# A convolution's reload moved one step behind its store, at two places of an LSTM, and the first chunk's work moved ahead in attention's opening

## The chip, the cores and the metric

The kernel runs on one core of one Trainium2 chip. A core has five engines with instruction queues of their own: PE (TensorE, matrix products), DVE (VectorE), ACT (ScalarE), POOL (GpSimd) and SP (SyncE, which here only issues transfers between the core's memory and DRAM). The metric is the device time of one execution in microseconds (us); less is better.

## The reference

The input x is [128, 64, 256]: 128 graphs of 64 nodes with 256 features, and one 64x64 adjacency for all. Four layers follow each other, each of the form x = x + layer(relu(layernorm(x))):

```
layer 0: two-layer perceptron with batch norms, after an aggregation with the normalized adjacency
layer 1: two graph convolutions
           h = relu(adj @ (h @ Wg0 + bg0)) ;  h = relu(adj @ (h @ Wg1 + bg1))
         then for p = 1, 2, 3, 4: an LSTM over windows of p nodes; its last state
         replaces the last node of each window
           g = x_t @ Wih.T + h @ Whh.T + bias ; c = sig(f) c + sig(i) tanh(g) ; h = sig(o) tanh(c)
layer 2: causal attention with one head, mask adj, output projection
layer 3: attention with four heads, masked where adj is 0
```

All is float32.

## The kernel before

**Tiling.** The 128 x 64 rows are cut into 16 chunks of 512 rows (NCH = 16), two chunks make a superchunk (SUP = 2), so there are 8 superchunks, sc = 0 to 7. Layer 0 runs first over all chunks. The stage in the middle runs over superchunks: the LSTMs of superchunk sc stand in it (`lstms`), and around them, as fillers, the convolutions of the next superchunk, the residual of the last one and the first steps of attention's norm. The last stage runs over chunks: attention of layer 2 for chunk c beside layer 3 for chunks c-1 to c-3.

**The order is written by hand.** In the middle stage the LSTM is a generator that stops at numbered marks: p=1 has marks 0 to 3, p=2 has 4 to 7, p=3 has 8 to 13, p=4 has 14 to 21, with half marks between. Tables of numbers say at which mark each step of a filler is taken: `FIRST` and `CONV` for the convolutions of the next superchunk (`FIRST` while sc = 0), `BEGUN` for the first steps of those of the superchunk after that (while sc is 0 to 5), `LATE` and `AHEAD` for the norm of attention. Each table has one tuple per chunk of the superchunk. So `BEGUN[0]` opens the convolution of its first chunk at marks 11, 11.5, ... and `BEGUN[1]` that of its second at 17.5, 19, 21.

**The convolution's filler** (`convolutions`). First step: the batch norm's scale and shift (L918). Second step: DVE transposes the chunk by 32x32 blocks into `ym` (L1009), a transfer stores it to DRAM as `far_y` (`put`, L261), four transfers reload it in another arrangement into `cv` (`get`, L268), and one loads x into `xs` (L1016); `xs` takes the place of `ym`. Third step: DVE adds both (`add_squares`, L298). Then come the layer norm's statistics in two steps (L195, L196, with POOL's rsqrt at L99, L100 and `nmr` at L202, L203), its application on ACT (L210), the aggregation, the product v (L936), the bound (L942), the product u (L950), the second aggregation and the copy to `hT` (L961).

**The LSTM's weights.** Sets of 896 KB (`wset`, one for each p and gate q) are reloaded for each superchunk, two at a time, into six buffers. `load_sets(2)` (L905) stands twice in the last step of each p: just behind the half mark (11.5 in p=3, 19.5 in p=4) and before the last mark (13 and 21). The two sets loaded behind mark 11.5 are those of p=4 for q=3 and q=1. The order of first products in p=4 is q=0, q=2 and q=3 (L1134; q=3 writes tile `x`).

**One queue for transfers.** All transfers of this stage are issued by SyncE in the order in which the program lists them. The transfer's wait (for a store's landing, or for a buffer to come free) is a wait of SyncE, so what is listed behind it is issued later.

**The single LSTM, p=1.** Three gates at once, products L1369, adds on DVE L1393, activations on ACT L1374 and L1382, copies L1389.

**Attention's opening.** The last stage begins with a string of step names, `FIRST` (a second use of that name), which interleaves chunks 0 to 3: `score2` (L1719, L1722, then `mx` L1642 and POOL's subtraction L1643), `exp2` (L1729), `divide2` (sum L1647, reciprocal L1652, product L1653), `turn2` (transposes L1662, copy L1666), `v2a` and `v2b` (L1521, L1523), `q2` (L1528, L1697) and `copyq2` (L1702), `out2` (products L1750, adds into `xs` L1753), `keep` (store `far_x`) and `back` (its reload), `weights3` (load of `w_sb`, whose memory is that of chunk 0's v), `norm3`, `apply3` (L187), `chan3` (transposes `tc_n` L240), `q3`, `k3` (L1528 with `w_sb`), `score3` (L1904, L1910), and for the last two chunks of layer 1 the residual `res1` (transposes `hm` L1309, store and reload `far_h`, add L298) and the reordering `pair1` (store and reload `far_n`). `load3+1` is the reload `hT` of chunk 1 for layer 3, whose first product is `Z` (L1825).

Of the kernel before, what the change touches and what calls it, by code (L numbers as in the profile page):

```python
# [19 lines left out]
def kernel(  # L20
# [169 lines left out]
    def norm_halves(src, name):  # L190

        st = small.tile([P, NJ, 6], F32, tag=f"ln_st{NJ}", name=f"st_{name}")
        mv = small.tile([P, NJ, 2], F32, tag=f"ln_mv{NJ}", name=f"mv_{name}")
        for j in range(NJ):
            nc.vector.bn_stats(st[:, j, :], src[:, j, :])  # L195
            nc.vector.bn_aggr(mv[:, j, :], st[:, j, :])  # L196
            if j == NJ // 2 - 1:
                yield
        rstd = small.tile([P, NJ], F32, tag=f"ln_rstd{NJ}", name=f"rstd_{name}")
        nmr = small.tile([P, NJ], F32, tag=f"ln_nmr{NJ}", name=f"nmr_{name}")  # L200
        rsqrt(rstd, mv[:, :, 1], EPS)
        nc.gpsimd.tensor_tensor(nmr, mv[:, :, 0], rstd, OP.mult)  # L202
        nc.gpsimd.tensor_scalar(nmr, nmr, -1.0, None, op0=OP.mult)  # L203
        yield rstd, nmr

    def apply_halves(dst, src, stats, name):

        rstd, nmr = stats
        for j in range(NJ):
            nc.scalar.activation(dst[:, j, :], src[:, j, :], AF.Relu, bias=nmr[:, j : j + 1],  # L210
                                 scale=rstd[:, j : j + 1])
            if j % 2:
                yield
# [4 lines left out]
    def aggregate(src, mat, name):  # L218

        banks = [bank(f"agg{e}_{name}").rearrange("p (k j t) -> p k j t", j=NJ, t=T) for e in range(2)]
        for j in range(NJ):
            for k in range(KD):
                for i in range(2):
                    for e in range(2):
                        f = slice(k * P + i * T, k * P + (i + 1) * T)
                        nc.tensor.matmul(banks[e][half(i), k, j, :], src[half(e), j, f],
                                         mat[half(e), half(e)], start=True, stop=True)
        return [ps.rearrange("p k j t -> p (k j) t") for ps in banks]  # L230
# [27 lines left out]
    def put(mid, name, tag="far", bufs=12):  # L258

        far = dram.tile([P, Q, CH * KD // Q], F32, tag=tag, name=f"far_{name}", bufs=bufs)  # L260
        nc.sync.dma_start(far, mid)  # L261
        return far

    def get(dst, far):

        src = far.rearrange("(a t) b n -> b t a n", a=Q)
        for b in range(Q):
            nc.sync.dma_start(dst[b * 32 : (b + 1) * 32], src[b])  # L268
# [21 lines left out]
    def add_squares(dst, base, src):  # L290

        for h in range(2):
            q = slice(h * Q // 2, (h + 1) * Q // 2)

            def part(a):
                return a.rearrange("p j (k q c) -> p q (j k) c", k=KD, q=Q)[:, q]

            nc.vector.tensor_add(part(dst), part(base), src[:, q].rearrange("p q (n c) -> p q n c", c=32))  # L298
# [613 lines left out]
    def scaled(y, c, m):  # L912
        one = slice(m, m + 1)
        if c == 0 and not m or c == 1:
            nc.scalar.activation(y[:, m, :], z2[c][:, m, :], AF.Identity, bias=sh2[:, one],
                                 scale=sc2[:, one])
        else:
            nc.vector.tensor_scalar(y[:, m, :], z2[c][:, m, :], sc2[:, one], sh2[:, one],  # L918
                                    op0=OP.mult, op1=OP.add)
# [4 lines left out]
    def conv_tile(c):  # L924

        t = shared(f"cv_{c}")
        return t.rearrange("p (k n) -> p k n", k=KD), t.rearrange("p (j d) -> p j d", d=D)

    def by_batch(agg):
        return agg.rearrange("p k (j e t) -> p e (k j) t", e=2, t=T)  # L930

    def product_v(c, agg):
        banks = [bank(f"v1_{c}_{m}") for m in range(KD)]
        for m in range(KD):
            for k in range(KD):
                nc.tensor.matmul(banks[m], wg0_sb[:, k, m * P : (m + 1) * P], agg[:, k, :],  # L936
                                 start=(k == 0), stop=(k == KD - 1))
        return banks

    def bounded(v, banks):  # L940
        for m in range(KD):
            nc.vector.tensor_tensor(v[:, m, :].rearrange("p (j n) -> p j n", n=P),  # L942
                                    banks[m].rearrange("p (j n) -> p j n", n=P),
                                    nc1[:, m, None, :].to_broadcast([P, NJ, P]), OP.max)

    def product_u(c, v):
        banks = [bank(f"u1_{c}_{t}").rearrange("p (j d) -> p j d", d=D) for t in range(NJ // 2)]
        for j in range(NJ):
            for k in range(KD):
                nc.tensor.matmul(banks[j // 2][:, j % 2, :], v[:, k, j * P : (j + 1) * P],  # L950
                                 wg1_sb[:, k, :], start=(k == 0), stop=(k == KD - 1))
        return banks

    def biased(u, banks):
        for t, ps in enumerate(banks):
            nc.vector.tensor_add(u[:, 2 * t : 2 * t + 2, :], ps, c2[:, None, :].to_broadcast([P, 2, D]))
# [44 lines left out]
    def convolutions(c):  # L1001

        y, h = conv_tile(c)
        for m in range(KD):
            scaled(y, c, m)
        yield
        mid = res.tile([P, Q, CH * KD // Q], F32, tag=f"r{c}", name=f"ym_{c}")
        for k in range(KD):
            nc.vector.transpose(  # L1009
                mid.rearrange("p b (j k c) -> p k j b c", j=NJ, k=KD)[:, k],  # L1010
                y[:, k, :].rearrange("p (j b t) -> p j b t", b=Q, t=32))
        far = put(mid, f"y{c}")
        dst = y.rearrange("p k (q n) -> p (k q) n", q=2)
        get(dst, far)
        xs[c] = res.tile([P, NJ, D], F32, tag=f"r{c}", name=f"xs_{c}")
        nc.sync.dma_start(xs[c], xr[c])  # L1016
        yield
        add_squares(xs[c], xs[c], dst)
        yield
        for stats in norm_halves(xs[c], f"b{c}"):  # L1020
            yield
        yield from apply_halves(h, xs[c], stats, f"b{c}")
        banks = aggregate(h, adjt_bd, f"b{c}")
        yield
        for e, ps in enumerate(banks):
            nc.vector.tensor_copy(by_batch(y)[:, e], ps)
        yield
        banks = product_v(c, y)
        yield
        bounded(y, banks)  # L1030
        yield
        banks = product_u(c, y)
        yield
        biased(h, banks)
        yield
        banks = aggregate(h, adjt_bd, f"c{c}")
        yield
        for e, ps in enumerate(banks):
            to_hT(c, e, ps)
            yield  # L1040
# [514 lines left out]
    EARLY = 0, 3, 5, 7, 9, 9, 13, 15  # L1555
    RESIDUAL = (0, 6, 9), (5.5, 7, 9.5)
    CONV = (3, 4, 5, 5.5, 7, 8, 9, 10, 10), (5, 5, 6, 9.5, 11, 11.5, 13, 14, 15, 15.5, 17, 18, 20)
    BEGUN = (11, 11.5, 14.5, 17, 17, 20, 21), (17.5, 19, 21)
    RESIDUAL_LAST = (0, 4, 5.5), (3, 5, 9)
    FIRST = (1, 1, 2, 2, 3, 4, 4, 5, 5.5, 7, 8, 9, 10, 10), (2, 3, 4.5, 5, 5, 6, 9.5, 11, 11.5, 13, 14, 15, 15.5, 17, 18, 20)  # L1560
    AHEAD = (9, 10), (10, 11)
    LATE = (4.5, 4.5, 5.5, 9, 19.5), (9.5, 9.5, 11, 12, 21)
    LATEST = (4.5, 4.5, 5.5, 9, 9.5), (9.5, 9.5, 10, 11, 11.5)
# [27 lines left out]
    with tc.manual_schedule(engines={mybir.EngineType.PE, mybir.EngineType.DVE, mybir.EngineType.Pool,  # L1591
# [4 lines left out]
        for sc in range(last + 1):  # L1596
            todo = {}

            def units(places, unit):
                for n in places:  # L1600
                    todo.setdefault(n, []).append(unit)


            if sc < last:
                for i in range(SUP):
                    units((CONV if sc else FIRST)[i], convs[(sc + 1) * SUP + i])
                new_hT(sc + 1)
# [11 lines left out]
            if sc + 1 < last:  # L1619
                for i in range(SUP):  # L1620
                    units(BEGUN[i], convs[(sc + 2) * SUP + i])
            if sc == last:
# [406 lines left out]
    def store(c, t):  # L2029
# [3 lines left out]
        for r in range(2):  # L2033
# [16 lines left out]

    FIRST = """load2+2 score2+0 exp2+0 res1+14 v2a+1 v2b+1 score2+1 divide2+0 load2+3 q2+2 copyq2+2
               turn2+0 exp2+1 v2a+2 out2+0 keep+0 divide2+1 norm3+0 v2b+2 turn2+1 score2+2 res1+15 out2+1
               keep+1 exp2+2 weights3+0 divide2+2 apply3+0 back+0 chan3+0 res1+14 turn2+2 res1+15 norm3+1
               q30+0 k30+0 out2+2 keep+2 res1+14 q31+0 res1+15 k31+0 apply3+1 pair1+14 pair1+14 square3+1
               score3+0 norm3+2 pair1+15 pair1+15 v3a+0 load3+1 v3b+0"""
    LAST = """exp3-2 sum3-2 load3+0 divide3-2 qa-1 q5-1 c11-1 v3a-1 qb-1 c12-1 qc-1 turn3-2 qd-1 out3-2
              score3-1 q30+0 store-2 back-1 k30+0 back+0 exp3-1 q31+0 sum3-1 k31+0 divide3-1 score3h+0
              v3b-1 exp3a+0 sum3a+0 turn3-1 exp3b+0 v3a+0 divide3a+0 out3-1 sum3b+0 divide3b+0 store-1  # L2060
# [8 lines left out]
    with tc.manual_schedule(engines={mybir.EngineType.PE, mybir.EngineType.DVE,  # L2069
                                     mybir.EngineType.Activation, mybir.EngineType.Pool,  # L2070
                                     mybir.EngineType.SP}):
        run(FIRST, 0)
        close_l1r()
# [61 lines left out]
```

## Time and profile before

| what | value |
|---|---|
| time, median of 3 runs | 1904.61 us (1903.06 to 1906.54) |
| span of the profiled execution | 1901.8 us |
| PE busy | 1845.0 us, 97% of the span |
| DVE, ACT, POOL busy | 1323.1, 1052.1, 613.0 us |
| chain that ended last, share of PE | 85% |
| layer 1's LSTM stage | about 274 to 1521 us |
| attention's opening | about 1521 to 1565 us |
| `wset` loads | 96, of 896 KB, median 8.2 us from issue to landing |
| `far_y`, `cv`, `xs` transfers | median 2.6, 3.0 and 4.5 us to landing |

Lines of the timeline read: start in us, busy time in us, engine, line of the kernel, operation, output <- inputs, shapes, count; in brackets how long the engine was idle before and what ended that. "SPq" is the issue of a transfer by SyncE. "PEld" is TensorE's weight load, which overlaps its products. A wait is put down to the releaser that came last by the profile.

### The profile page before, as it was taken

The page shows a single profiled execution, that of the slowest core. Times are in us where ns is not written, and L with a number is a line of the kernel's source. Part 1 is how long each engine was busy: PE and PEld are TensorE (multiplying, and loading weights), DVE is VectorE, ACT ScalarE, POOL GpSimd, SP SyncE. Part 2 cuts the span into 40 slices and gives each one's busy share as a digit, 9 for nine tenths or more (in the row PEclk, how much of TensorE's full clock was granted, in tenths as well). Part 3 has the DMA queues.
Part 4 walks back from the last instruction along what each step waited for, and adds up shares of the span by engine and source line. Part 5 has one row for each costly group of instructions (what it writes and reads, how often), then busy time and mean ns, then how long its engine had stood idle before and what let it go on. Part 6 is the DMA issues. An engine that isn't in the chain of part 4 may idle for free.

```text
span 1901.8 us, 40668 instructions
## 1 busy us (share of the span) xinstructions
PE 1845.0 (97%) x15463; PEld 1519.0 (80%) x15463; DVE 1323.1 (70%) x3408; ACT 1052.1 (55%) x2499; POOL 613.0 (32%) x856
## 2 busy tenths in 40 slices
PE   8999988999999999999999999999999989999998
PEld 6877856987987888799698788789979956777776
DVE  6768846667667777776776776876667666776776
ACT  5766545546547456564664655656556534444453
POOL 5856632223213322222422322332222213332232
PEclk9999999999999999999999999999999989999999
DMA  3224551123433343242343334333244155454433
GB/s 114 79 66 145 207 205 53 62 109 122 149 118 123 111 156 118 89 130 87 133 156 112 145 122 145 145 103 131 95 123 145 35 161 145 139 152 144 135 112 112
DMA packets 113410, 234.48 MB, mean 123 GB/s; under 512 B 11712, under 2 KB 77120, under 8 KB 113216
## 3 DMA queue, kind: packets, MB, share of 16 engines
q1 hardware_dynamic: 112320, 230.02, 36.4%
q8 instruction: 123, 2.02, 0.4%
q0 software_dynamic: 320, 1.05, 0.2%
q10 hardware_dynamic: 576, 0.82, 0.1%
q14 instruction: 71, 0.58, 0.1%
HBM read 164.21 MB, written 67.63 MB: 122 GB/s over the span
## 4 chain that ended last, share of the span: by engine, by line
PE 85%; DVE 6%; DMA 3%; ACT 2%; POOL 2%; issue 1%; SPq 0%; DVEq 0%; ACTq 0%; POOLq 0%
PE x L1187 21%; PE z L1187 11%; PE y L1187 6%; PE v L1521 5%; PE y L1134 4%; PE x L1369 4%; PE y L1369 3%; PE u L950 3%; PE x L1134 3%; PE p_q L1528 3%; PE X L1825 3%; PE X L437 2%; DMA wset<-wfar 2%; PE X L513 2%; PE v L936 2%; PE z L1134 2%
## 5 line engine op out<-in xcount | busy, mean ns | idle before, releaser
L1102 ACT ACTIVATE l_gates<-l_gates,bias 128x256 f32<-128x256 f32 (+4 forms) x528 | 238.1, 498 | 217.3 <-DVE l_gates L1196 109.9
L1187 PE MATMUL x<-xd,wset 128*128 128x128 f32 (+2 forms) x1152 | 255.0, 303 | 0.8 <-ACT l_gates L1193 0.8
L1187 PE MATMUL x<-l_hd,wset 128*128 128x128 f32 (+2 forms) x1152 | 254.5, 303 | 0.0
L1253 POOL TENSOR_TENSOR l_gates<-l_gates 128x512 f32<-128x512 f32 (+2 forms) x48 | 75.3, 1569 | 397.8 <-ACT l_gates L1102 397.8
L1187 PEld LDWEIGHTS x<-xd,wset 128*128 128x128 f32 x1152 | 187.7, 191 | 6.5 <-issue 1.4
L1187 PEld LDWEIGHTS x<-l_hd,wset 128*128 128x128 f32 x1152 | 187.8, 191 | 5.0
L1196 DVE TENSOR_TENSOR l_gates<-l_gates,x 128x128 f32<-128x128 f32 (+2 forms) x384 | 121.1, 321 | 97.4 <-PE x L1187 94.4
L1196 DVE TENSOR_TENSOR l_gates<-l_gates,z 128x128 f32<-128x128 f32 (+2 forms) x384 | 102.3, 318 | 106.8 <-PE z L1187 104.7
L1187 PE MATMUL z<-l_hs,wset 128*128 128x128 f32 (+2 forms) x768 | 147.1, 304 | 0.7 <-DVE l_hs L1111 0.7
L1187 PE MATMUL z<-hT,wset 128*128 128x128 f32 (+2 forms) x768 | 146.2, 303 | 0.0
L1193 ACT COPY l_gates<-y 128x128 f32<-128x128 f32 (+2 forms) x192 | 53.2, 290 | 137.6 <-PE y L1187 131.3
L1187 PEld LDWEIGHTS z<-l_hs,wset 128*128 128x128 f32 x768 | 116.8, 191 | 5.8 <-DVE l_hs L1111 2.5
L1187 PEld LDWEIGHTS z<-hT,wset 128*128 128x128 f32 x768 | 117.1, 191 | 3.3
L1102 ACT ACTIVATE l_gates<-x,bias 128x128 f32<-128x128 f32 (+2 forms) x216 | 84.8, 393 | 28.9 <-PE x L1187 26.2
L1187 PE MATMUL x<-hT,wset 128*128 128x128 f32 (+2 forms) x384 | 85.8, 305 | 0.0
L1187 PE MATMUL x<-l_hs,wset 128*128 128x128 f32 (+2 forms) x384 | 84.8, 303 | 0.0
L327 POOL TENSOR_TENSOR xd<-hT 128x128 f32<-128x128 f32 (+2 forms) x72 | 42.7, 594 | 126.6 <-DVE hT L1113 114.3
L1187 PE MATMUL y<-l_hd,wset 128*128 128x128 f32 (+2 forms) x384 | 83.2, 309 | 0.0
L1187 PE MATMUL y<-xd,wset 128*128 128x128 f32 (+2 forms) x384 | 81.6, 304 | 0.0
L1268 ACT ACTIVATE l_gates<-l_cell 128x256 f32<-128x256 f32 (+2 forms) x144 | 55.3, 384 | 45.5 <-DVE l_cell L1267 45.5
L1643 POOL TENSOR_TENSOR s<-s,mx 128x256 f32<-128x256 f32 (+2 forms) x33 | 40.5, 1226 | 122.6 <-DVE mx L1642 122.6
L1141 DVE TENSOR_TENSOR l_gates<-l_gates,y 128x256 f32<-128x256 f32 (+2 forms) x144 | 46.4, 343 | 46.5 <-PE y L1134 42.9
(356 smaller groups left out, 4593.5 us busy)
## 6 DMA issues: line engine op xcount, KB each, us to landing
wset<-wfar SPq DMA_DIRECT2D x96, 896.0 KB, 8.2
hT<-far_h SPq DMA_DIRECT2D x124, 128.0 KB, 3.8
far_h<-hm SPq DMA_DIRECT2D x16, 512.0 KB, 3.0
far_n<-xs SPq DMA_DIRECT2D x16, 512.0 KB, 3.1
xs<-far_n SPq DMA_DIRECT2D x64, 128.0 KB, 2.8
far_x<-xs SPq DMA_DIRECT2D x16, 512.0 KB, 2.9
x<-far_x SPq DMA_DIRECT2D x64, 128.0 KB, 3.4
xt<-in_x_dram SPq DMA_DIRECT2D x15, 512.0 KB, 3.9
```

Source lines behind the costliest of these rows:

```text
L950: nc.tensor.matmul(banks[j // 2][:, j % 2, :], v[:, k, j * P : (j + 1) * P], wg1_sb[:, k, :], start=(k == 0), stop=(k == KD - 1))
L1102: nc.scalar.activation(gate(q, c, part), src, AF.Tanh if q == 2 else AF.Sigmoid, bias=bs[:, q * KD + c : q * KD + c + 1])
L1134: nc.tensor.matmul(folded(self.psum(kind)), wsets[p, self.q][:, BLOCKS[kind][0], :], ox[0][kind], start=kind in (1, 5), stop=True, skip_gr ...
L1187: nc.tensor.matmul(folded(self.psum(kind)), wsets[p, self.q][:, BLOCKS[kind][i], :], (ox[self.s] if part == "x" else oh)[kind], start=firs ...
L1193: nc.scalar.copy(gate(self.q, kind // 5, halves[kind // 5]), self.psum(kind))
L1196: nc.vector.tensor_add(gate(self.q, *dst), gate(self.q, *a), self.psum(kind))
L1253: nc.gpsimd.tensor_mul(gates[:, 0, :, :n], gates[:, 0, :, :n], gates[:, 2, :, :n])
L1268: nc.scalar.activation(gate(2, c, part), cells[:, c, part], AF.Tanh)
L1369: nc.tensor.matmul(folded(ps(g, kind)), single_block(KINDS1[kind])[:, g, :], right[kind], start=kind in (2, 5, 1), stop=True, skip_group_c ...
L1521: nc.tensor.matmul(ps[:, i, :], hT[:, k, j, :], w[:, k, first : first + D], start=(k == 0), stop=(k == KD - 1))
L1528: nc.tensor.matmul(ps.rearrange("p (a n) -> p a n", n=P), w[:, k, m * P : (m + 1) * P], hT[:, k], start=(k == 0), stop=(k == KD - 1))
L1825: nc.tensor.matmul(st[c, tag][:, i * CH // 2 : (i + 1) * CH // 2].rearrange("p (a n) -> p a n", n=P), w, st[c, "o7"][kind], start=first an ...
```

## The change

It has two parts. In `convolutions` one `yield` is added between the store and the reload, which makes the reload (and the load of x) a step of its own; the tables get one number more per chunk for it. The store stays where it was, and the reload goes to mark 13 (from 11.5) and to mark 20 (from 19), so that the weight loads listed in between are issued ahead of it and do not stand behind the wait for the store's landing. In `FIRST`, for superchunk 0, the reloads are at marks 0 and 4; chunk 2's second statistics come at mark 1 (before: 2), chunk 3's add at 5 (before: 4.5) and its second statistics at 5.5 (before: 5).

In attention's opening the steps of chunk 0 (`divide2`, `turn2`, `out2`, `keep`, `norm3`) and the load of layer 3's weights are listed ahead of chunk 2's `q2` and of chunk 1's scores; `chan3+0`, `turn2+2` and `out2+2` come ahead of `q30` and `k30`; and the residual's steps of chunks 14 and 15 are put later. The operations are the same ones.

```diff
         far = put(mid, f"y{c}")
+        yield
         dst = y.rearrange("p k (q n) -> p (k q) n", q=2)
         get(dst, far)
...
-    BEGUN = (11, 11.5, 14.5, 17, 17, 20, 21), (17.5, 19, 21)
+    BEGUN = (11, 11.5, 13, 14.5, 17, 17, 20, 21), (17.5, 19, 20, 21)
...
-    FIRST = (1, 1, 2, 2, 3, 4, 4, 5, 5.5, 7, 8, 9, 10, 10), (2, 3, 4.5, 5, 5, 6, 9.5, 11, 11.5, 13, 14, 15, 15.5, 17, 18, 20)
+    FIRST = (0, 1, 1, 1, 2, 3, 4, 4, 5, 5.5, 7, 8, 9, 10, 10), (2, 3, 4, 5, 5, 5.5, 6, 9.5, 11, 11.5, 13, 14, 15, 15.5, 17, 18, 20)
...
-    FIRST = """load2+2 score2+0 exp2+0 res1+14 v2a+1 v2b+1 score2+1 divide2+0 load2+3 q2+2 copyq2+2
-               turn2+0 exp2+1 v2a+2 out2+0 keep+0 divide2+1 norm3+0 v2b+2 turn2+1 score2+2 res1+15 out2+1
-               keep+1 exp2+2 weights3+0 divide2+2 apply3+0 back+0 chan3+0 res1+14 turn2+2 res1+15 norm3+1
-               q30+0 k30+0 out2+2 keep+2 res1+14 q31+0 res1+15 k31+0 apply3+1 pair1+14 pair1+14 square3+1
-               score3+0 norm3+2 pair1+15 pair1+15 v3a+0 load3+1 v3b+0"""
+    FIRST = """load2+2 score2+0 exp2+0 v2a+1 v2b+1 divide2+0 score2+1 turn2+0 load2+3 v2a+2 exp2+1 res1+14
+               out2+0 keep+0 weights3+0 q2+2 norm3+0 divide2+1 v2b+2 copyq2+2 turn2+1 score2+2 apply3+0 back+0
+               out2+1 keep+1 exp2+2 chan3+0 divide2+2 res1+15 res1+14 turn2+2 norm3+1 out2+2 keep+2 q30+0
+               k30+0 res1+15 q31+0 k31+0 apply3+1 res1+14 res1+15 pair1+14 square3+1 score3+0 norm3+2
+               pair1+14 pair1+15 v3a+0 load3+1 v3b+0 pair1+15"""
```

Against the kernel before, the listed order of SyncE's transfers at the first place becomes store, four weight loads, reload, x; at the second place it becomes store, (`far_n` of another chunk), two weight loads, reload, x, two weight loads. The listed order of PE and ACT changes in the opening alone.

## The prediction

> **What bounds the kernel now.** I read the page first. TensorE is busy 97% of the span and makes 85% of the chain that ended last, so only what stops TensorE, or slows it, can pay. The waits of TensorE, longest first, say where it stops (engine, line, what it waited for; us in total, times, longest):
>
> ```profile
> PE x L1134 <- DMA wset<-wfar: 14.9, 6, 3.4
> PE x L1134 <- ACT l_gates L1374: 5.4, 1, 5.4
> PE tc_n L240 <- ACT h L187: 5.1, 1, 5.1
> PE Z L1825 <- DMA hT<-far_h: 3.0, 1, 3.0
> ```
>
> All four lie where the change works. The first is a load of LSTM weights, met once in each of superchunks 0 to 5 as p=4 opens. The timeline of superchunk 1:
>
> ```profile
> 379.27 0.32 SPq L261 DMA_DIRECT2D far_y<-ym  x1
> 382.02 1.74 SPq L268 DMA_DIRECT2D cv<-far_y  x4
> 383.81 0.43 SPq L1016 DMA_DIRECT2D xs<-in_x_dram  x1
> 384.34 2.31 SPq L905 DMA_DIRECT2D wset<-wfar  x4
> 384.86 3.60 PE L936 MATMUL v<-cv,wg_sb 128*128 128x512 f32 x8
> 388.29 0.61 PE L1134 MATMUL y<-hT,wset 128*128 128x128 f32 x4
> 391.17 0.76 PE L1134 MATMUL x<-hT,wset 128*128 128x128 f32 x2 [2.27 <-DMA wset<-wfar]
> ```
>
> The store far_y goes out at 379.27; SyncE then stands until it has landed (382.02), needs 1.74 us to issue the reload and 0.43 for x, and only then, at 384.34, issues the weights, though the first two buffers were free at about 378, when TensorE's last products with them ended. The wait is not all: the windows show the clock after it (last three columns: granted clock, DMA share, GB/s).
>
> ```profile
> 392.00:394.00 2.00, 2.00 (x11) 2.00 (x11) 0.29 (x1) 1.03 (x4) 1.65 (x4) 0.50 1.05 441
> ```
>
> Superchunk 6 has no such store and shows what the stretch costs undisturbed, from the v products to the u products:
>
> ```profile
> 1320.21 3.60 PE L936 MATMUL v<-cv,wg_sb 128*128 128x512 f32 x8
> 1329.75 1.46 PE L950 MATMUL u<-wg_sb,cv 128*128 128x256 f32 x6
> ```
>
> That is 9.54 us. Between the same marks superchunks 0 to 5 take 13.60, 13.57, 12.28, 14.69, 14.15 and 11.80. Last, attention's opening:
>
> ```profile
> 1542.56 0.32 SPq L261 DMA_DIRECT2D far_x<-xs  x1
> 1542.98 0.41 SPq L1972 DMA_DIRECT2D w_sb<-in_w_dram  x1
> 1544.30 2.80 PE L240 MATMUL tc_n<-ident,h 128*128 128x128 f32 x8 [5.11 <-ACT h L187]
> 1548.96 2.04 PE L1528 MATMUL p_q<-hT,w_sb 128*128 128x512 f32 x2 [1.44 <-DVE st_n L159]
> 1576.75 1.10 PE L1825 MATMUL Z<-hT,w_sb 128*128 128x256 f32 x4 [3.03 <-DMA hT<-far_h]
> ```
>
> The weights w_sb are issued at 1542.98, behind far_x of chunk 1, and take 5.8 us to land: 1548.8. So the wait at 1548.96, put down to DVE, was this load. In the window 1539 to 1549 TensorE is busy 3.41 of 10 us at a mean clock of 0.62.
>
> **What the Trainium skill says.** "DMA: Bandwidth & Descriptors", Queues, rings and completion order: each SDMA engine consumes a queue's descriptors in ring order, and completion need not be in order. The trace agrees on landings: four weight sets issued from 384.34 on landed 6.7, 8.3, 10.1 and 11.5 us after their issues, about 2.2 us apart, the first 2.7 after xs. "TensorE: Matmul & The Clock Gate", Part 1: the clock is halved after an idle stretch and comes back after some microseconds of work; the trace agrees (0.50 after a 2.27 us wait). The same page, Architectural detail, calls ACT and DVE strict FIFO, which is how a late reload can hold the LSTM's own adds.
>
> **Part 1: first reload (mark 11.5 to 13).** Nothing is added or removed on any engine but the order of SyncE: store, four weight loads, then reload and x. Weights for q=3 are issued at about 379.7 in place of 384.34. The store lands at 382.0, so at 2.2 us a set the two wanted sets land near 384.3 and 386.5; TensorE asks for the first at 388.29 + 0.45 = 388.74. The wait goes, and the slow clock with it. Gain: 80.09 (the six stretches) - 6 x 9.54 = 22.8 us. New wait: the reload now queues behind two loads that wait for the end of p=3's products (about 385). They land near 389.5 and 391.7, cv near 393.3, xs near 395.0. The add that reads them (L298) stood at 399.94 and moves up to 399.94 - 4.06 = 395.9, just after: no cost.
>
> **Part 2: second reload (mark 19 to 20).** The two weight sets that overtake it are not wanted for 20 us, so there is nothing to gain here, and the reload comes later. In superchunks 2 to 5 the queue also holds a store far_n that waits for DVE's nm. Before, superchunk 2:
>
> ```profile
> 745.12 1.99 SPq L268 DMA_DIRECT2D cv<-far_y  x4
> 747.15 0.43 SPq L1016 DMA_DIRECT2D xs<-in_x_dram  x1
> 755.08 2.51 DVE L298 TENSOR_TENSOR xs<-xs,cv 128x512 f32<-128x512 f32 x2
> 757.51 1.27 DVE L1393 TENSOR_TENSOR l_gates<-l_gates,x 128x512 f32<-128x512 f32 x2
> 758.22 1.33 ACT L1374 ACTIVATE l_gates<-l_gates,bias 128x512 f32<-128x512 f32 x2 [2.44 <-DVE l_gates L1393]
> ```
>
> After: far_n at 745.5 (nm is done at 745.4), landing near 748.4; two sets near 750.6 and 752.9; cv near 754.5; xs 756 to 756.7. L298 wanted them at 755.08, so DVE stands 0.9 to 1.6 us. Behind it on DVE is L1393, for which ACT and TensorE already wait (TensorE 0.24 us at 758.84). With a little of the slow clock I take 1.5 us in each of four superchunks: +6 us. Both ends: 0, if xs lands as fast as the 4.3 us seen elsewhere, and 3 each (12). In superchunks 0 and 1 there is no far_n: landing near 444.2 for L298 at 443.30, and TensorE has about 1 us in hand there (L1393 begins at 445.84, its bank is next written at 447.68). Nothing.
>
> **Part 3: superchunk 0.** Chunk 2's second statistics come before the LSTM's y adds. ACT's L210 waited 3.62 us for POOL's nmr (297.64), and TensorE 5.43 us for the ACT work behind it (300.46). Now nmr is ready near 292; but two pairs of statistics (1.17 us) go ahead of L1393, so ACT's preceding L1374 ends at 294.03 + 1.17 = 295.2, and L210 starts there and not at 297.64. Gain 2.4. Chunk 3's later add and statistics lie in DVE's idle time (1.29 us at 323.98).
>
> **Part 4: the opening.** No work is added. DVE: division of chunk 0 ends near 1527.9, before the transpose hm (2.1 us) and not after. TensorE: turn 1528.1, v 1528.5 to 1530.3, out2(0) to 1531.4, then q2. DVE adds to 1532.8, so far_x and w_sb go out by 1533.2 and land by 1539: that wait is gone. Statistics to 1535, nmr near 1539.3 (behind the mask of chunk 2, whose scores end at 1538.1), ACT's apply 1539.4 to 1541.5, TensorE's tc_n to 1542.9, turn and out2(2) to 1546.2, with idle pieces of some 1 us. Then q3, k3 start at 1546.2 and not 1548.96, with out2(2) already done, which stood between them before: 16 products at 0.43 us, ending 1553.1 warm, about 2 us later if the clock is still half (window 1549 to 1565.3 before: 0.82). Scores and v bring q2 of chunk 3 to 1558.2 (cold 1560) against 1565.35. The next limit is DVE: its mask moves from 1564.09 to 1558.1, hence the division (ends 1577.8) to about 1571.8, and the transposes behind it to end at 1572.4 against 1581.5. The reload hT for Z now precedes the second xs reload and lands near 1566, when TensorE arrives (1566.5). Gain 9.1 warm, 7 cold; I take 8.
>
> **Sum.** 1904.6 - 22.8 + 6 - 2.4 - 8 = 1877.4 us.
>
> **Rivals.**
> A. Part 2 costs nothing (SyncE finds the rings empty, xs lands in 4.3 us) and the opening runs warm: -22.8 - 2.4 - 9.1 gives 1870. For it: DMA is 0.60 busy around 746. Against it: 2 x 2.2 us of weights stand ahead. 0.22.
> B. The late reload costs 3 us in each of four and 1 in two superchunks (14), and the opening gives 4 because out2, now ahead of q3, waits for ACT's copy: -22.8 - 2.4 + 14 - 4 = 1889. For it: xs landed 6.2 us after issue in superchunk 3. 0.18.
> C. Slower: the first place only swaps waits. If the two sets did not get their buffers at 379 but at 385, the reload, behind all four, would hold DVE at L298 at both places, 12 x 2 us = 24, with no gain in part 1 and 2.4 + 8 elsewhere: 1918. Against it: TensorE's last use of those buffers is at 378. 0.03.
> My forecast, within about 5 us: 0.57. The ends of A and B bound the unknown costs, so the range is 1866 to 1891. Faster 0.96, same 0.01, slower 0.03.
>
> **What would show it.** Right: no wait of x L1134 for wset; v to u near 9.5 us in six superchunks; a new DVE wait at L298 for xs at the ends of superchunks 2 to 5, about 1.5 us, and a TensorE gap after it; w_sb issued near out2(0); q2 of chunk 3 about 7 us sooner after the LSTM's end. Wrong: weights still landing after 388.7 in the same place; L298 held also at the first place; q3 waiting for something other than w_sb.

## The result, and the profile after

| kernel | median us | lowest to highest | runs |
|---|---|---|---|
| before | 1904.74 | 1901.47 to 1907.37 | 20 |
| changed | 1899.49 | 1894.53 to 1908.78 | 20 |

The ratio is 0.9975, with a 95% interval of 0.9964 to 0.9986. The change makes the kernel faster, by about 5 us (0.25%), where the forecast was 27 us. The direction was right, and the size was far off, outside the range. In the changed kernel's trace every line behind L1012 has a number higher by one (L1134 is L1135, L1369 is L1370, L1393 is L1394).

The waits of TensorE in the changed kernel (engine, tile, line, what it waited for; us in total, times, longest):

```profile
PE x L1370 <- DVE l_gates L1394: 17.6, 7, 3.7
PE z L1188 <- DVE l_hs L1112: 6.5, 6, 2.0
...
PE x L1135 <- ACT l_gates L1375: 1.7, 1, 1.7
...
PE tc_n L240 <- ACT h L187: 1.1, 4, 0.7
PE Z L1826 <- DMA hT<-far_h: 1.1, 1, 1.1
```

All four waits that were shown of before have gone or become small: 14.9 us for `wset` is gone, 5.4 became 1.7, 5.1 became 1.1, 3.0 became 1.1. Two new ones stand on top, 24.1 us together, and both name DVE. (One of the seven waits at L1370, 1.43 us at 292.80, belongs to superchunk 0, where the statistics now go ahead of L1394 as Part 3 of the forecast had it. The other six stand at the second place.) What DVE waited for stands in its own list:

```profile
DVE xs L298 <- DMA xs<-in_x_dram: 33.7, 11, 4.8
```

In the kernel before that row was absent. The end of the chain has moved with it: here is its part by engine and by line on the page of the changed kernel.

```profile
PE 80%; DMA 6%; DVE 6%; ACT 3%; issue 2%; SPq 2%; POOL 2%; DVEq 0%; ACTq 0%; POOLq 0%
```

Before, it read PE 85%, DMA 3%. So one transfer, the weights, was taken off the path, and another, the load of x behind the reload, was put on it.

**The same place as before, the first reload of superchunk 0.** (The forecast calls this stretch superchunk 1; by the numbering of the kernel it is superchunk 0, as p=1 of superchunk 1 begins only at 439.95 in the kernel before.) The timeline of the changed kernel:

```profile
374.53 0.32 SPq L261 DMA_DIRECT2D far_y<-ym  x1
374.94 5.68 SPq L905 DMA_DIRECT2D wset<-wfar  x4
380.12 3.60 PE L936 MATMUL v<-cv,wg_sb 128*128 128x512 f32 x8
380.72 2.44 SPq L268 DMA_DIRECT2D cv<-far_y  x4
383.21 0.44 SPq L1017 DMA_DIRECT2D xs<-in_x_dram  x1
383.99 0.39 PE L1135 MATMUL x<-hT,wset 128*128 128x128 f32 x2
...
394.46 1.29 DVE L298 TENSOR_TENSOR xs<-xs,cv 128x512 f32<-128x512 f32 x2 [3.30 <-DMA xs<-in_x_dram]
395.67 0.42 DVE L1167 TENSOR_TENSOR l_cell<-l_gates 128x256 f32<-128x256 f32 x1
396.12 0.42 ACT L1168 ACTIVATE l_gates<-l_cell 128x256 f32<-128x256 f32 x1 [4.11 <-DVE l_cell L1167]
396.57 0.42 DVE L1112 TENSOR_TENSOR l_hs<-l_gates 128x256 f32<-128x256 f32 x1 [0.48 <-ACT l_gates L1168]
397.05 1.16 PE L1188 MATMUL z<-l_hs,wset 128*128 128x128 f32 x8 [1.99 <-DVE l_hs L1112]
```

The upper half is what was forecast: weights ahead of the reload, no wait at the x products. The lower half is the new cost. `xs` is issued at 383.21 and lands 11.1 us later; DVE stands at L298 for 3.30 us, and behind it in DVE's order stands L1167, a step of the LSTM's cell. ACT, then DVE again, then TensorE each wait for it in turn. TensorE loses 1.99 of the 3.30 us, so about 1.3 us of slack lay in the chain here.

**The second reload, superchunk 2.** Timeline of the changed kernel:

```profile
738.31 0.33 SPq L261 DMA_DIRECT2D far_n<-nm  x1
738.75 1.19 SPq L905 DMA_DIRECT2D wset<-wfar  x2
740.35 2.22 SPq L268 DMA_DIRECT2D cv<-far_y  x4
742.61 0.55 SPq L1017 DMA_DIRECT2D xs<-in_x_dram  x1
...
752.25 1.29 DVE L298 TENSOR_TENSOR xs<-xs,cv 128x512 f32<-128x512 f32 x2 [4.22 <-DMA xs<-in_x_dram]
753.46 1.28 DVE L1394 TENSOR_TENSOR l_gates<-l_gates,x 128x512 f32<-128x512 f32 x2
754.18 1.33 ACT L1375 ACTIVATE l_gates<-l_gates,bias 128x512 f32<-128x512 f32 x2 [5.52 <-DVE l_gates L1394]
754.29 4.51 PE L1370 MATMUL x<-xd,wih 128*128 128x512 f32 x6 [3.13 <-DVE l_gates L1394]
```

DVE would have begun at 748.03 (752.25 - 4.22) and TensorE stops for 3.13 us. Its six products then take 4.51 us, where six took 2.74 at 743.27. The windows (first column behind the comma: busy time of TensorE; last three columns: granted clock, DMA share, GB/s) say why, and what the transfers were doing:

```profile
746.00:748.00 2.00, 2.00 (x7) 0.80 (x6) 2.00 (x6) 2.00 (x6) 1.69 (x2) 1.00 1.10 218
748.00:750.00 2.00, 2.00 (x6) 0.95 (x5) 0.03 (x1) 0.66 (x2) 1.92 (x3) 1.00 1.13 200
750.00:752.00 2.00, 1.16 (x3) 0.19 (x1) 0.00 (x0) 0.00 (x0) 0.81 (x1) 1.00 1.09 395
...
751.44:754.85 3.41, 0.56 (x2) 0.35 (x3) 2.60 (x5) 0.67 (x2) 0.00 (x0) 1.00 1.01 416
754.85:758.27 3.42, 3.42 (x6) 1.36 (x5) 2.66 (x6) 3.42 (x8) 1.28 (x1) 0.50 0.43 174
```

The clock is at 0.50 after the wait. That is so in superchunks 2 and 5 alone. In superchunk 3 the wait is longer and the six products behind it are fast:

```profile
913.79 2.81 PE L1370 MATMUL x<-xd,wih 128*128 128x512 f32 x6 [3.71 <-DVE l_gates L1394]
...
908.46:911.87 3.41, 1.62 (x4) 0.38 (x2) 0.12 (x1) 0.00 (x0) 1.26 (x1) 1.00 1.08 356
911.87:915.29 3.42, 1.50 (x4) 0.81 (x5) 3.42 (x7) 1.61 (x3) 0.20 (x1) 1.00 1.00 409
915.29:918.70 3.41, 3.41 (x10) 1.49 (x9) 2.66 (x6) 3.41 (x8) 1.09 (x1) 1.00 0.38 151
```

Why the two differ is taken up in the last section.

While the reload and x move, from 746 to 750, the 16 engines are busy throughout yet move only 200 to 218 GB/s, half of the 395 that they reach when the next weights move.

**Where the time went, by stage.** Each row is the sum of the six superchunks from one group of products to the next (first products of v, u, p=1 and p=2), or one stretch:

| stretch | before | changed | difference | forecast |
|---|---|---|---|---|
| v to u (first place, weights) | 80.1 | 58.2 | -21.9 | -22.8 |
| u to p=1 (first place, L298) | 249.2 | 256.4 | +7.2 | 0 |
| p=1 to p=2 (second place, L298) | 116.4 | 136.3 | +19.8 | +6 |
| first v of superchunk 0 to first v of superchunk 1 | 59.9 | 55.4 | -4.5 | -2.4 |
| opening, last u to the end | 572.0 | 564.0 | -8.0 | -8 |
| sum | | | -7.4 | -27.2 |

The profiled spans, 1901.8 and 1894.1 us, differ by 7.7.

### The profile page after: what moved, and what is told of

It reads as the page before. It is cut to its first block, busy times and chain, and to the rows that moved or that the text cites. A ratio compares the mean times of both kernels' runs of the same rounds, so it can differ in the third digit from the quotient of the medians.

```text
span 1894.1 us, 40658 instructions
## 1 busy us (share of the span) xinstructions
PE 1840.2 (97%) x15463; PEld 1511.4 (80%) x15463; DVE 1318.7 (70%) x3408; ACT 1048.1 (55%) x2499; POOL 608.5 (32%) x856
## 3 DMA queue, kind: packets, MB, share of 16 engines
q8 instruction: 123, 2.02, 0.4%
## 4 chain that ended last, share of the span: by engine, by line
PE 80%; DMA 6%; DVE 6%; ACT 3%; issue 2%; SPq 2%; POOL 2%; DVEq 0%; ACTq 0%; POOLq 0%
PE x L1188 21%; PE z L1188 10%; PE y L1188 6%; DMA xs<-in_x_dram 6%; PE v L1522 5%; PE y L1135 3%; PE x L1370 3%; PE p_q L1529 3%; PE X L1826 3%; PE x L1135 2%; PE X L437 2%; PE v L936 2%; PE u L950 2%; PE X L513 2%; PE y L1370 1%
## 5 line engine op out<-in xcount | busy, mean ns | idle before, releaser
L1370 PE MATMUL x<-xd,wih 128*128 128x512 f32 x144 | 68.5, 622 | 17.6 <-DVE l_gates L1394 17.6
```

Source lines behind the costliest of these rows:

```text
L1370: nc.tensor.matmul(folded(ps(g, kind)), single_block(KINDS1[kind])[:, g, :], right[kind], start=kind in (2, 5, 1), stop=True, skip_group_c ...
```

## The experiments

My theory (Theory 1) was that the weight sets issued ahead of a reload make it land late, and that at the second place, where nothing was gained by it, this cost some 20 us. The rivals put the loss on the later mark itself, on the `far_n` store, or on the other parts. Ratios are to the kernel before, run beside: 1902.72 us for the first four runs, 1904.18 for the last four.

**First place alone, and second place alone.** In the first kernel the second reload goes back to mark 19; in the second, the first reload goes back to 11.5.

```diff
-    BEGUN = (11, 11.5, 13, 14.5, 17, 17, 20, 21), (17.5, 19, 20, 21)
+    BEGUN = (11, 11.5, 13, 14.5, 17, 17, 20, 21), (17.5, 19, 19, 21)     # first place alone
+    BEGUN = (11, 11.5, 11.5, 14.5, 17, 17, 20, 21), (17.5, 19, 20, 21)   # second place alone
```

> The second reload is put back beside its store (mark 19); the rest is the changed kernel. Theory 1 (the second reload lands late because weight sets go ahead of it in the queue, and DVE's add holds the LSTM): the stretch from p=1's first product to p=2's first shrinks from 21.0-24.3 us to 19.2-19.5 us in superchunks 1 to 6, DVE waits for xs in six places and not in eleven, and the time falls by about 19.8 us from 1899.5 to about 1880. Theory 2 (the loss in p=1 comes from the earlier weights at the first place, which shift the DRAM traffic): p=1 keeps its 21 to 24 us and the time stays near 1899.

> The first reload is put back beside its store (mark 11.5), the second stays at mark 20. Theory 1: the six waits of x for wset come back (v to u 11.8 to 14.7 us, 21.9 us in all), the waits of z for l_hs go (7.2 us), the loss in p=1 stays: about 1899.5 + 21.9 - 7.2 = 1914 us, slower than the kernel before by about 10. Theory 2: p=1 back at 19.2-19.5 us, time about 1894.

Measured: 1879.96 us for the first (ratio 0.9879, 0.9863 to 0.9894) and 1911.34 for the second (1.0044, 1.0028 to 1.0061). TensorE's waits in the kernel with the second place alone:

```profile
PE x L1370 <- DVE l_gates L1394: 17.8, 7, 3.8
PE x L1135 <- DMA wset<-wfar: 15.1, 6, 3.5
```

The old wait is there and the new one on top: p=1 to p=2 sums to 136.4, as in the changed kernel (136.3), and to 116.4 where the second reload is at mark 19. The second place's move costs about 20 us and gives nothing. The first place keeps the gain (v to u: 57.7), but u to p=1 sums to 262.1, a loss of 12.9 where the changed kernel had 7.2. The reason is in the waits of L298 there, 15.8 us in six (1.54 to 3.96) against 13.4 in the changed kernel, and in what the clock makes of them: it is halved behind two of the six here, and behind none in the changed kernel. After a TensorE wait of 0.23 eight products take 1.16 us, after one of 2.65 they take 2.08 (timeline of the kernel with the first place alone):

```profile
395.49 1.16 PE L1188 MATMUL z<-l_hs,wset 128*128 128x128 f32 x8 [0.23 <-DVE l_hs L1112]
...
550.16 2.08 PE L1188 MATMUL z<-l_hs,wset 128*128 128x128 f32 x8 [2.65 <-DVE l_hs L1112]
```

"TensorE: Matmul & The Clock Gate" of the Trainium skill, Part 1, has the clock halved after an idle window of about 3.4 us, and has these windows run freely, whatever the kernel does. Here a wait of 2.65 us was enough (the window of 550 to 552 shows 0.50). Around 2 us it goes either way: after 1.99 us in the changed kernel the eight took 1.16, after 1.89 elsewhere in this run 1.84. The traces agree with the free windows, and these decide between the two, as the last section shows.

**How many sets stand ahead of the second reload.** The mark stays at 20, but the weights behind mark 19.5 are moved to the end of p=4, both of them (none ahead) or one (one ahead). The edit for one ahead, where SKIP is 4; for none ahead the first call is left out while p is 4, and the 3 is a 4:

```diff
             if last:
-                load_sets(2)
+                load_sets(2 if p < SKIP else 1)
...
             if last:
-                load_sets(2)
+                load_sets(2 if p < SKIP else 3)
                 ending()
```

> The changed kernel with the two weight sets of mark 19.5 in p=4 moved to the end (four sets at mark 21, none ahead of the reload); the reload stays at mark 20. Theory 1 (the sets ahead in the queue make the second reload late): cv is issued about 1.6 us sooner and no set is in flight with it, so xs lands before L298 wants it, p=1's stretch goes back from 136 to about 117 us in the sum of the six superchunks, and the time is near 1880. Theory 2 (the later mark itself, or the far_n store ahead of it, is what costs): L298 still waits for xs by over 3 us in each superchunk and the time stays near 1897.

> The changed kernel with one weight set ahead of the second reload instead of two (three at mark 21). Theory 1 in its simple form (each set ahead delays the reload by its own 2.5 to 3 us): the wait of DVE L298 falls from about 4.2 to 1.5 us, the PE wait behind it from 3.1 to about 0.5, p=1's stretches sum to 120 to 123, time near 1885. Rival (the delay does not come by the set, but from the reload sharing the engines with whatever set is in flight): L298 still waits over 3 us and the time is 1893 or more.

Measured: none ahead 1877.2 us (ratio 0.9853, 0.9831 to 0.9875), one ahead 1885.05 (0.9894, 0.9867 to 0.9920), beside the changed kernel's 1899.49 with two. In superchunk 2 of each:

| sets ahead | xs, issue to landing | wait of DVE L298 | p=1 to p=2 there | the six |
|---|---|---|---|---|
| 0 | 5.2 us | none | 19.50 | 116.5 |
| 1 | 7.9 | 1.75 | 20.99 | 122.6 |
| 2 | 9.5 | 4.22 | 24.28 | 136.3 |

The two lines of L298 (timelines, none ahead and one ahead):

```profile
745.65 2.52 DVE L298 TENSOR_TENSOR xs<-xs,cv 128x512 f32<-128x512 f32 x2
```

```profile
744.69 2.18 DVE L298 TENSOR_TENSOR xs<-xs,cv 128x512 f32<-128x512 f32 x2 [1.75 <-DMA xs<-in_x_dram]
```

With no set ahead the stage is back to what it was before the change (19.50 us in superchunk 2 both times, and 116.5 against 116.4 in the six), with the same mark and the same `far_n` store ahead. So neither the mark nor the store alone costs anything; the sets do. The store seems to matter only with them, though no run takes it away: in superchunks 0 and 1, which have none, one set costs 0.3 and 0.0 us and two cost 1.8 and 1.9, while in 2 to 5 one costs 1.4 to 1.5 and two cost 3.1 to 4.8. The second set costs more than the first: slack hides part of the first, and in superchunks 2 and 5 the slow clock follows the second.

**The reload in another queue.** The second place's reload and x are issued by POOL; SyncE keeps the weights.

```diff
-            nc.sync.dma_start(dst[b * 32 : (b + 1) * 32], src[b])
+            (queue or nc.sync).dma_start(dst[b * 32 : (b + 1) * 32], src[b])
...
-        get(dst, far)
+        queue = nc.gpsimd if c % SUP and c >= 2 * SUP else nc.sync
+        get(dst, far, queue)
...
-        nc.sync.dma_start(xs[c], xr[c])
+        queue.dma_start(xs[c], xr[c])
```

> The changed kernel with the second place's reload cv and x load xs issued by POOL instead of SyncE, so that they are in another queue than the two weight sets; same mark. If the order within one queue is the delay, the reload shares the engines with the sets from its issue and lands in about 6 us, L298 waits under 2 us, and the time is 1880 to 1888. If the 16 engines serve what was issued first whatever its queue, xs lands as late as before and the time stays near 1899. If POOL's own issue is dear (POOL's L1118 and L328 stand behind it), the time is above 1899.

Measured: 1931.18 us (ratio 1.0139, 1.0118 to 1.0161), slower than any other. The issues of superchunk 2, and what followed (timeline):

```profile
747.93 5.11 SPq L905 DMA_DIRECT2D wset<-wfar  x4
749.54 2.27 POOL L268 DMA_DIRECT2D cv<-far_y  x4
751.80 0.79 POOL L1018 DMA_DIRECT2D xs<-in_x_dram  x1
755.53 0.70 POOL L1119 TENSOR_TENSOR hT<-l_gates 128x128 f32<-128x128 f32 x1 [2.94 <-ACT l_gates L1270]
...
765.72 1.29 DVE L298 TENSOR_TENSOR xs<-xs,cv 128x512 f32<-128x512 f32 x2 [8.48 <-DMA xs<-in_x_dram]
```

The time is that of the third expectation, but not for its reason. POOL's later work does not stand behind its issues: POOL is idle for 2.94 us, waiting for ACT, before its next work at 755.53. But `xs` now lands 13.8 us after its issue. Two things come together. The first packet of POOL's queue moves at 753.5, 3.9 us after POOL begins to issue. And with the reload out of SyncE's list, SyncE issues all four sets in one stretch, and the reload shares the engines with four sets instead of queuing behind two. "DMA: Bandwidth & Descriptors" of the Trainium skill, Queues, rings and completion order, has each SDMA engine take turns between queues packet by packet. The trace agrees: from 754 to 764 it has 318 packets of POOL's queue (1.00 MB) beside 325 of SyncE's (2.10 MB). The order within one queue had been protecting the reload from the last two sets. How much of the 13.8 us is the late start of POOL's queue and how much the sharing, no run separates.

**The opening alone, and superchunk 0 alone.** The kernel before with the new string `FIRST` of attention; and the kernel before with the new table of superchunk 0 (the new `yield` is there, both reloads at their stores' marks).

```diff
-    BEGUN = (11, 11.5, 13, 14.5, 17, 17, 20, 21), (17.5, 19, 20, 21)
+    BEGUN = (11, 11.5, 11.5, 14.5, 17, 17, 20, 21), (17.5, 19, 19, 21)   # and the old opening: superchunk 0 alone
```

> The kernel before with the new order of attention's opening alone. If the opening's gain of 8 us, read from the two traces behind the last u product, is its own: 1904.7 - 8 = about 1897. If it came from the reload's move (other phase of the clock or of the queue at the LSTM's end): about 1904.

> The kernel before with the changed table of superchunk 0 alone (reload right behind its store at both places, the old opening). If part 3 acts by itself, the stretch of superchunk 0 shortens by 4.5 us as in the changed kernel and the time is near 1898; if the 4.5 us needed another part of the change, by 2.4 us or less: 1900 to 1902.

Measured: the opening alone 1893.85 us (ratio 0.9953, 0.9940 to 0.9966), 8.9 us less than before. Superchunk 0 alone 1898.52 us (0.9972, 0.9962 to 0.9982), 5.7 less. Both act by themselves.

**A version that keeps the gain without the loss.** The second reload stays at mark 19. The first goes to mark 12, between the two pairs of weights, so that two sets are ahead of it and not four.

```diff
-    BEGUN = (11, 11.5, 13, 14.5, 17, 17, 20, 21), (17.5, 19, 20, 21)
+    BEGUN = (11, 11.5, 12, 14.5, 17, 17, 20, 21), (17.5, 19, 19, 21)
```

> The first reload between the two pairs of weight sets (mark 12 in place of 13), the second beside its store (mark 19). Theory 1: the wanted weights still land in time (v to u 9.5 us), and the reload has two sets ahead of it and not four, so xs lands about 5 us sooner, before DVE wants it: no wait of DVE for xs, u to p=1 back at 41.5 us, and about 1880 - 7 = 1873 us. If instead the reload's lateness is SyncE's own (the issue, not the queue ahead), DVE still waits 1 to 3 us for xs and the time is that of the run with the first place alone.

Measured: 1868.13 us (ratio 0.9816, 0.9804 to 0.9828), faster than both kernels. Its timeline at the first place of superchunk 0:

```profile
374.03 0.32 SPq L261 DMA_DIRECT2D far_y<-ym  x1
374.44 1.21 SPq L905 DMA_DIRECT2D wset<-wfar  x2
377.14 2.04 SPq L268 DMA_DIRECT2D cv<-far_y  x4
379.23 0.47 SPq L1017 DMA_DIRECT2D xs<-in_x_dram  x1
379.74 0.98 SPq L905 DMA_DIRECT2D wset<-wfar  x2
...
390.64 1.29 DVE L298 TENSOR_TENSOR xs<-xs,cv 128x512 f32<-128x512 f32 x2
```

SyncE issues the two sets while the store is on its way and then waits only for the rest of its flight. The reload goes out 3.1 us after its store, not 6.2 us as in the changed kernel, and L298 has no wait. v to u sums to 57.6, u to p=1 to 249.2, p=1 to p=2 to 116.4: the gain of the first place with none of the losses.

## Why the prediction was right in direction and wrong in size

- **Part 1, the weights: right.** 22.8 us forecast, 21.9 measured. The x products no longer wait, and v to u is 9.54 to 9.90 us in every superchunk.
- **Part 1, "just after: no cost": wrong.** It measured 7.2 us, and 12.9 in the run with the first place alone; L298 held at the first place was one of the forecast's own signs of being wrong. The order was right, the landings were not, and only 0.9 us had been left between the landing of xs (395.0) and the add (395.9). On the changed kernel's clock the forecast has the last two sets at 384.8 and 387.0, cv at 388.6 and xs at 390.3 (its times less 4.74, by which v begins sooner). They came at 386.1, 388.9, about 391.8 and 394.3. So the last set is 1.9 us late, and the step from the last set to xs took 5.4 us and not 3.3. L298 was wanted at 391.16, as forecast.
- **Part 2, the main error.** The forecast saw the mechanism (the sets overtake the reload, L298 waits, L1393 stands behind it) and named what would show it; what failed is the size, 1.5 us in each of four superchunks, and "Nothing" in superchunks 0 and 1. Counted from the issue of `far_n`, it put the two sets at 5.1 and 7.4 us and xs at 10.5 to 11.2. They came at 6.4, 10.0 and 13.8 (744.7, 748.3 and 752.1). L298 was wanted at 9.7, as forecast at 9.6. The mis-sized term is the "2.2 us a set", which I took from a stretch where sets followed sets. Here the first set was 1.3 us late, and the second came 3.6 us after it. The four 128 KB pieces of the reload were issued between 740.35 and 742.6, while the sets were still in flight, and the rate fell to 218 GB/s. That the sharing with small packets made the second set late is read from the trace; no run changes it alone. The 4.2 us wait of DVE became 3.13 of TensorE and, with the slow clock, 4.8 us of the stage; in superchunks 3 and 4, at full clock, the stage lost 3.7 and 3.1. So about 1.1 us of slack lay here, where the forecast saw none: the 0.24 us at 758.84 that it read as a wait of TensorE is idle time of the weight load, and the products run on beside it. Superchunks 0 and 1 lost 1.8 and 1.9 us. Sum +19.8 for +6.
- **Its upper bound was too low as well.** "3 each (12)" is below the 3.1 to 4.8 measured in superchunks 2 to 5, and it left out the two superchunks without `far_n`. The rival with 14 us there was nearer. The loss side of the slower rival, 24 us of waits at L298 at both places, came true and more: the twelve waits sum to 36.4 us, and the two stretches lost 27.0. Its premise, that the first two sets get no buffers, did not.
- **Part 3: the steps right, the sum too small.** L210 was put at 295.2 and stands at 295.38. TensorE's wait for ACT fell from 5.43 to 1.70 us, and the x products begin 2.3 us sooner (298.17 for 300.46). What was left out is that the long wait had also slowed the products behind it: before, the four z products take 1.91 us, now 1.03. In the windows the granted clock is 0.74 and 0.69 over 296 to 308 before, and 1.00 over 292 to 304 now. That makes 4.5 where 2.4 were forecast, and 5.7 alone.
- **Part 4: right in its steps up to q3 and k3, and in its sum.** The forecast has `w_sb` issued by 1533.2, tc_n done at 1542.9 and q3, k3 from 1546.2 on, perhaps with a slow clock. The timeline of the changed kernel:

```profile
1532.86 0.34 SPq L261 DMA_DIRECT2D far_x<-xs  x1
1533.30 0.38 SPq L1973 DMA_DIRECT2D w_sb<-in_w_dram  x1
1541.32 0.77 PE L240 MATMUL tc_n<-ident,h 128*128 128x128 f32 x5 [0.16 <-ACT h L187]
1546.59 3.74 PE L1529 MATMUL p_q<-hT,w_sb 128*128 128x512 f32 x4
1550.16 1.89 PE L1529 MATMUL p_k<-hT,w_sb 128*128 128x512 f32 x4
```

The first four products at 3.74 us, twice the next four's 1.89, are the slow clock for which the forecast allowed 2 us. Measured 8.0 us in the profile and 8.9 alone. Behind q3 and k3 less was gained than forecast: q2 of chunk 3 begins 4.8 us sooner (1560.54 for 1565.35; about 7 were named) and Z comes at 1569.99, not at 1566.5. That the sum still met the 8 us is in part luck, as 0.9 us of it came only later in the last stage.

- **The direction and the range.** The direction held because the gains (21.9, 4.5 and 8.0) outweighed losses of 27.0 that had been put at 6. As for the range, its parts were bounded one by one, but both errors of Parts 1 and 2 have one cause, the time that transfers need when they share the engines, and so they went the same way.

## What to carry to other kernels

When a transfer is moved behind others in a queue, ask of every transfer that is overtaken who waits for it last and how much slack that has. Size its landing from a stretch where the same kinds of transfer are in flight together: here big weight sets alone came 2.2 us apart, and 3.6 us apart with a fine-grained reload beside them. A move that helps at one place should not be repeated at another where the overtaking loads are not urgent; here it gained nothing there and cost 20 us. And a wait of TensorE of about 3 us cost its own length at full clock (3.71 us of wait, 3.7 of the stage) and half as much again where the clock was halved behind it (3.13 and 4.8), so the same wait can be worth either, on the side of the gains as on that of the losses.

## What was not expected of the hardware

- Full engines need not mean full rate. With the reload (four pieces of 128 KB) and x in flight, all 16 engines were busy (share 1.10 and 1.13) at 200 to 218 GB/s, against 395 GB/s with weight sets; in the run with no set ahead it was 224 from 738 to 742 (share 0.92 and 1.08), as the reload and x went first. The packets differ. Two lines of the changed kernel, for 746 to 750 and for 752 to 754:

```profile
DMA packets 859, 0.84 MB, mean 209 GB/s; under 512 B 66, under 2 KB 855, under 8 KB 859
DMA packets 133, 0.84 MB, mean 419 GB/s; under 512 B 16, under 2 KB 16, under 8 KB 133
```

The same 0.84 MB took 859 packets and 4 us while the reload and x moved, and 133 packets and 2 us with weight sets. No run changes the size of the packets alone.

- In this kernel a second queue was no way past a busy one: from POOL's queue, `xs` needed 13.8 us beside four sets, against 9.5 behind two sets in SyncE's queue and 5.2 with none ahead.
- The length of a wait does not tell whether the clock is halved after it: 1.89 us did it once, 3.71 us did not. The granted clock changes on a grid. In each trace all starts of half clock lie a whole number of steps of 3.413 us apart (in the changed kernel 754.85 and 1225.89, 138 steps; with the first place alone 549.97 and 1014.18, 136 steps), and half clock lasts one such step or several. Half clock goes with how long TensorE is busy within the step before. The wait of 3.13 us lies nearly whole in the step from 751.44, which has 0.56 us of work, and the next step is at 0.50. The wait of 3.71 us is shared by two steps that keep 1.62 and 1.50 us of work, and the clock stays at 1.00. With the first place alone the wait of 1.89 us falls into one step from 1010.77 with 1.52 us of work, and the next is at 0.50; the 1.99 us of the changed kernel is shared by steps with 2.02 and 2.81 us. Over the ten traces, leaving out the step in which the program begins, a step at full clock with less than 1.4 us of work was always followed by half clock, and one with more than 2.0 us never; between them it went either way. The grid does not begin with the program: in the changed kernel's trace it lies 1.4 us off that of the kernel before (298.85 there). So part of what a short wait costs is chance.
